# Self-attention and the ternary layers of a perceiver's second level as one part, tile by tile

## The chip, the cores and the metric

The kernel runs on one core of a Trainium2 chip. The metric is the device time of one execution in microseconds (us); lower is better. TensorE is PE in the profile (its weight loads are PEld), VectorE is DVE, ScalarE is ACT, GpSimd is POOL, and SyncE, SP, issues nearly all transfers.

## The reference

Two levels of a perceiver run over tokens x of (8, 64, 512), each with a cross-attention to a context of (8, 1601, 512). Only the end of the second level is touched:

```python
x = x + _L1_xattn_ref(_layernorm(x), ctx_1024, ctx_1024, ...)
x = x + _L1_attn_ref(_layernorm(x), Wq, Wk, Wv, u, v, Wo, bo)
x = x + _L1_ffn_ref(_layernorm(x), w1, b1, w2, b2)
```

`_L1_attn_ref` is a self-attention over the 64 tokens of a batch with 16 heads of 32 and relative positions. The scores are `(q + u) kT + rel_shift((q + v) rT)`, times 32^-0.5, where r are sinusoids of the position. `rel_shift` pads a row of 64 with one zero, reads the rows of 65 as one run of numbers, and takes rows of 64 from it, one row later. A softmax, the values and the product with Wo (plus bo) follow. `_L1_ffn_ref` is two layers, 512 to 2048 to 512, with a gelu between them. Each normalizes its input by its root mean square, rounds it to integer levels of -128 to 127 by the row's largest value, and multiplies with weights rounded to -1, 0 and 1.

## The kernel before

The 512 tokens lie as four tiles of 128 (two batches each) in one buffer x. The tail has two functions that run one after the other.

`l1_attn` (L1545) first fills qv and qu, both 128x4096, with zeros on POOL (L1577, L1578). It normalizes the four tiles (`K.layernorm`: bn_stats, aggregate and variance on DVE at L71, L72, L55, a power on POOL at L56, the result xn on DVE at L76) and turns them into columns xT (xt_ps, L88). Then come the queries of all four tiles at once (q_ps L1587, 512 columns). Two heads share 64 partitions, and one product computes both heads' scores. So a query is stored twice, with zeros in the other head's half: qv on ACT (L1591) and qu on DVE (L1594), in pieces of 32x512 that leave the zeros where the fill put them. `of_pairs` (L1605) multiplies qv with the positions (y_ps); for each tile a zero column is set (L1617), the result is copied to y (two buffers), and four transfers write it to one DRAM buffer, shift, in rows of 65 (L1622). `while_shifting()` then loads the rounded weights w1q and w2q (L1778, L1780). Four transfers for each tile read the rows back in rows of 64 as z (L1637). While this runs, PE computes the keys (k_ps L1645) and values (v_ps L1650) of all tiles. After that, for each tile: `probabilities` (scores s_ps by `of_pairs`, the add of z L1659, max L1663, subtraction L1664, exp on ACT L1665, sum L1666, reciprocal, product L1668), `turn` (pT_ps L1677), `attend` (o_ps L1687, copies oT L1698) and `out` (out_ps L1704, x + bo L1711, x + out_ps L1712). The loop runs one tile ahead: probabilities(t+1) comes before the rest of tile t.

`l1_ffn` (L1806) begins when that is done. It loads the biases b1 and b2, and normalizes all tiles. `first(t)` makes levels of the row (`rms_levels`, L1784 to L1801: the square on ACT, the largest value and the passes on DVE, the root on POOL), turns them (xT_ps L1831), multiplies with w1q (h_ps L1837), scales and adds b1 (h L1840), applies gelu (L1843), and makes levels hq of the 2048 values. `second(t)` turns these (hT_ps L1854), multiplies with w2q (o_ps L1858), scales, adds b2 and x (L1860, L1861) and writes the tile out (L1862). The loop puts first(t) before second(t-1).

Nothing else orders the work by hand. Buffers come from pools, and a pool that is closed gives its memory to the next one; an instruction that writes into such memory waits for the last reader of what lay there. A planner with estimated costs puts the instructions of each engine into one order, and on each engine they run in that order. SP issues transfers in order as well, and an issue that has to wait keeps the later ones back.

What comes just ahead is the end of `l1_xattn`: sums and weighted values (L1465, acc L1456), their reciprocal (L1466) and product oT (L1529), the last tile's out_ps (L1471) and x + out_ps (L1478).

Of the kernel before, what the change touches and what calls it, by code (L numbers as in the profile page):

```python
# [10 lines left out]
F32 = mybir.dt.float32  # L11
# [1204 lines left out]
def l1_xattn(K, x, d):  # L1216
# [7 lines left out]
    with ExitStack() as es:  # L1224
        ep = es.enter_context(tc.tile_pool(name="d_e", bufs=1))
        cp = es.enter_context(tc.tile_pool(name="d_c", bufs=5))
        qp = es.enter_context(tc.tile_pool(name="d_sq", bufs=4))
        wp = es.enter_context(tc.tile_pool(name="d_w", bufs=1))
# [26 lines left out]
        wv = chunked(wp, "L1x_WvT")  # L1255
# [278 lines left out]
def positions():  # L1534

    pos = np.arange(S - 1, -1, -1, dtype=np.float32)
    inv = (1.0 / 10000.0 ** (np.arange(0, DH, 2, dtype=np.float32) / np.float32(DH))).astype(np.float32)
    ang = (pos[:, None] * inv[None, :]).astype(np.float64)
    r = np.concatenate([np.sin(ang), np.cos(ang)], axis=-1).astype(np.float32)
    return {"c_rT": np.tile(r.T, (4, 1))}  # L1540


def l1_attn(K, x, d, while_shifting):

    tc, nc = K.tc, K.nc
    with ExitStack() as es:
        wp = es.enter_context(tc.tile_pool(name="e_w", bufs=1))  # L1550
        rp = es.enter_context(tc.tile_pool(name="e_r", bufs=2))
        dp = es.enter_context(tc.tile_pool(name="e_d", bufs=1, space=DRAM))
        pm = es.enter_context(tc.tile_pool(name="e_ps", bufs=7, space=PSUM))

        qp = tc.tile_pool(name="e_q", bufs=1)
        q_pool = qp.__enter__()

        def weight(name, shape, src, pool=wp):
            t = pool.tile(shape, F32, tag=name, name=name)
            nc.sync.dma_start(t, src)  # L1560
            return t

        def chunked(name, pool=wp):
            return weight(name, [P, DC, D], d[name].rearrange("(c p) n -> p c n", p=P), pool)

        wq = chunked("L1a_Wq", q_pool)
        uv = weight("L1a_uv", [P, 2, DC], d["L1a_uv"])
        rT = weight("c_rT", [P, S], d["c_rT"])
        wk, wv, wo = chunked("L1a_Wk"), chunked("L1a_Wv"), chunked("L1a_Wo")
        bo = weight("L1a_bo", [P, D], bcast_rows(d["L1a_bo"]))  # L1570
        shift = dp.tile([B, 2, DC, 2, S * (S + 1)], F32, tag="shift", name="shift")

        xT = wp.tile([P, DC, B * S], F32, tag="xT", name="xT")

        qu = wp.tile([P, DC, B, 2, S], F32, tag="qu", name="qu")
        qv = q_pool.tile([P, DC, B, 2, S], F32, tag="qv", name="qv")
        nc.gpsimd.memset(qv, 0.0)  # L1577
        nc.gpsimd.memset(qu, 0.0)  # L1578
        xn = q_pool.tile([P, NT, D], F32, tag="xn", name="xn")
        K.layernorm(rp, x, xn)  # L1580
        K.tokens_to_columns(pm, "mm", xn, xT)
        uvs = wp.tile([P, 2, DC], F32, tag="uvs", name="uvs")
        nc.vector.tensor_scalar_mul(uvs, uv, DH**-0.5)
        for c in range(DC):
            ps = pm.tile([P, B * S], F32, tag="mm", name="q_ps")
            for i in range(DC):
                nc.tensor.matmul(ps, lhsT=wq[:, i, ts(c, P)], rhs=xT[:, i, :], start=i == 0, stop=i == DC - 1)  # L1587
            for i in range(4):
                r = ds(DH * i, DH)
                q = ps[r].rearrange("p (b q) -> p b q", b=B)  # L1590
                nc.scalar.activation(  # L1591
                    qv[r, c, :, i % 2, :], q, AF.Identity, bias=uvs[r, 1, c : c + 1], scale=DH**-0.5
                )
                nc.vector.tensor_scalar(  # L1594
                    qu[r, c, :, i % 2, :], q, uv[r, 0, c : c + 1], DH**-0.5, ALU.add, ALU.mult
                )

        def of_pairs(t, qb, rhs, name):

            halves = [pm.tile([P, DC, 2, S], F32, tag="mm", name=name) for _ in range(2)]  # L1600
            for c in range(DC):
                for b in range(2):
                    for j in range(2):
                        r = ds(64 * j, 64)
                        nc.tensor.matmul(  # L1605
                            halves[j][:, c, b, :],
                            lhsT=qb[r, c, 2 * t + b].rearrange("p h q -> p (h q)"),
                            rhs=rhs(r, c, 2 * t + b),
                            start=True,
                            stop=True,  # L1610
                        )
            return halves

        for t in range(NT):
            y = rp.tile([P, 2, DC, 2, S + 1], F32, tag="y", name="y")
            halves = of_pairs(t, qv, lambda r, c, b: rT[r], "y_ps")
            nc.gpsimd.memset(y[:, :, :, :, 0:1], 0.0)  # L1617
            for j in range(2):
                K.copy(y[:, j, :, :, 1:], halves[j])
            for b in range(2):  # L1620
                for h in range(2):
                    nc.sync.dma_start(  # L1622
                        shift[2 * t + b, :, :, h, :].rearrange("j c (q k) -> q (j c) k", k=S + 1),
                        y[ds(64 * h, 64), :, :, b, :].rearrange("q j c k -> q (j c) k"),
                    )

        qp.__exit__(None, None, None)
        while_shifting()
        bp = es.enter_context(tc.tile_pool(name="e_b", bufs=1))
        kT = bp.tile([P, DC, B * S], F32, tag="kT", name="kT")  # L1630
        v = bp.tile([P, NT, D], F32, tag="v", name="v")
        shifted = []
        for t in range(NT):
            z = bp.tile([P, 2, 2, DC, S], F32, tag=f"z{t}", name=f"z{t}")
            for b in range(2):
                for h in range(2):
                    nc.sync.dma_start(  # L1637
                        z[ds(64 * h, 64), b].rearrange("q j c k -> q (j c) k"),
                        shift[2 * t + b, :, :, h, S:].rearrange("j c (q k) -> q (j c) k", k=S),
                    )  # L1640
            shifted.append(z)
        for c in range(DC):
            ps = pm.tile([P, B * S], F32, tag="mm", name="k_ps")
            for i in range(DC):
                nc.tensor.matmul(ps, lhsT=wk[:, i, ts(c, P)], rhs=xT[:, i, :], start=i == 0, stop=i == DC - 1)  # L1645
            K.copy(kT[:, c, :], ps)
        for t in range(NT):
            ps = pm.tile([P, D], F32, tag="mm", name="v_ps")
            for i in range(DC):
                nc.tensor.matmul(ps, lhsT=xT[:, i, ts(t, P)], rhs=wv[:, i, :], start=i == 0, stop=i == DC - 1)  # L1650
            K.copy(v[:, t, :], ps)

        def probabilities(t):

            z = shifted[t].rearrange("p b j c k -> p j c b k")
            p = rp.tile([P, 2, DC, 2, S], F32, tag="p", name="p")
            halves = of_pairs(t, qu, lambda r, c, b: kT[r, c, ds(b * S, S)], "s_ps")
            for j in range(2):
                nc.vector.tensor_add(p[:, j], halves[j], z[:, j])  # L1659
            rows = p.rearrange("p j c b k -> p (j c b) k")  # L1660
            m = rp.tile([P, 16], F32, tag="m", name="m")
            wide = m.unsqueeze(2).to_broadcast([P, 16, S])
            nc.vector.tensor_reduce(m, rows, AX.X, ALU.max)  # L1663
            nc.vector.tensor_sub(rows, rows, wide)  # L1664
            nc.scalar.activation(rows, rows, AF.Exp)  # L1665
            nc.vector.tensor_reduce(m, rows, AX.X, ALU.add)  # L1666
            nc.vector.reciprocal(m, m)
            nc.vector.tensor_mul(rows, rows, wide)  # L1668
            return p

        def turn(p):

            pT = rp.tile([P, 2, DC, P], F32, tag="pT", name="pT")
            for j in range(2):
                ps = pm.tile([P, DC, P], F32, tag="mm", name="pT_ps")
                for c in range(DC):
                    nc.tensor.transpose(ps[:, c, :], p[:, j, c].rearrange("p b k -> p (b k)"), K.ident)  # L1677
                K.copy(pT[:, j], ps)
            return pT

        def attend(t, pT):
            o = [pm.tile([P, DC, 2, S], F32, tag="mm", name="o_ps") for _ in range(2)]
            for c in range(DC):
                for j in range(2):
                    for b in range(2):
                        r = ds(64 * b, 64)
                        nc.tensor.matmul(  # L1687
                            o[b][ds(64 * j, 64), c].rearrange("p h q -> p (h q)"),
# [299 lines left out]
```

## Time and profile before

| | us |
|---|---|
| median of 3 runs | 3331.86 (3327.32 to 3334.03) |
| the profiled execution | 3328.13 |
| its span | 3326.4 |
| end of the last out_ps of the cross-attention | 3106.13 |
| first q_ps | 3119.23 |
| first s_ps | 3171.74 |
| last x + out_ps of the attention (start) | 3239.10 |
| last out-add (start) | 3322.48 |
| from 3106 to 3327: PE, DVE, ACT, POOL busy | 141.11, 120.61, 55.12, 17.71 |
| the same stretch: granted clock | 0.78 |
| mean granted clock of the whole span | 0.974 |

The times in the lower rows are counted from the span's start. A row of the chain or of a timeline gives start, duration, engine, name and line, and how many instructions it holds. In a group's row, the numbers after the bar are the busy time, the mean duration of one instruction in ns, and the engine's idle time just before them with what ended it. A float32 product shows as two rows on PE (16 products of q_ps are 32 rows). The granted clock is the share of full speed that the throttle left to TensorE. Of the kernel's span, 3106 us lie ahead of the change.

### The profile page before, as it was taken

What the parts mean: (1) busy time and instruction counts of PE and PEld (TensorE: products, weight loads), DVE (VectorE), ACT (ScalarE), POOL (GpSimd) and SP (SyncE); (2) the same over time, 40 slices, a digit from 0 to 9 for tenths busy, and PEclk for the clock granted to TensorE, in tenths of its full rate; (3) what the DMA queues carried; (4) which work ended last, traced back from release to release, by engine and by line L of the source; (5) the groups of instructions that cost most, each with busy time, mean ns of one, the idle gap of its engine ahead of it and who ended that gap; (6) DMA issues with size and microseconds to landing.
All of it is one profiled execution on the core that took longest, in us unless ns stands there. A gap on an engine that the chain in (4) does not pass through costs nothing.

```text
span 3326.4 us, 40358 instructions
## 1 busy us (share of the span) xinstructions
PE 3171.3 (95%) x15812; PEld 2145.6 (65%) x15817; DVE 1773.4 (53%) x2931; ACT 837.0 (25%) x1530; POOL 1009.0 (30%) x974
## 2 busy tenths in 40 slices
PE   8999999999999999999899998999999999999765
PEld 6777778888878888875554444655555565555432
DVE  5754556666576656644432235454644545456546
ACT  3232322222233222201021221322223232232213
POOL 5433345443545444420000052313123141221100
PEclk9999999999999999998899998999999999999877
DMA  7255553333364343325388420010000100000430
GB/s 233 75 166 155 171 165 101 101 98 101 111 187 142 99 133 102 91 83 212 134 309 288 162 75 30 10 40 10 31 31 10 40 10 31 21 11 33 95 44 15
DMA packets 314178, 329.03 MB, mean 99 GB/s; under 512 B 35381, under 2 KB 235573, under 8 KB 312837
## 3 DMA queue, kind: packets, MB, share of 16 engines
q1 hardware_dynamic: 310272, 314.88, 30.6%
q10 hardware_dynamic: 3717, 11.57, 0.9%
q8 instruction: 126, 2.06, 0.2%
q14 instruction: 63, 0.52, 0.0%
HBM read 303.30 MB, written 23.10 MB: 98 GB/s over the span
## 4 chain that ended last, share of the span: by engine, by line
PE 87%; DVE 6%; DMA 3%; issue 1%; ACT 1%; POOL 1%; SPq 0%; ACTq 0%; POOLq 0%; DVEq 0%
PE k_ps L1293 11%; PE v_ps L1392 11%; PE x_ps L562 9%; PE x_ps L447 9%; PE s_ps L1406 4%; PE z_ps L562 4%; PE z_ps L447 4%; PE h_ps L1114 3%; PE oe_ps L1141 3%; PE acc L1456 3%; PE y_ps L562 2%; PE y_ps L447 2%; PE sum_ps L1315 2%; PE s_ps L440 1%; PE v_ps L595 1%
## 5 line engine op out<-in xcount | busy, mean ns | idle before, releaser
L1330 POOL TENSOR_TENSOR r<-r,minus_half 128x24 f32<-128x24 f32 x64 | 288.7, 4515 | 748.9 <-DVE r L1326 748.9
L1392 PE MATMUL v_ps<-L1x_WvT,ctxT 128*128 128x512 f32 (+1 forms) x832 | 380.1, 605 | 0.0
L1293 PE MATMUL k_ps<-ctxT,L1x_WkT 128*128 128x384 f32 (+1 forms) x1024 | 375.0, 509 | 0.6 <-ACT o L51 0.6
L447 PE MATMUL x_ps<-qt,ctxT 128*128 128x256 f32 x1152 | 285.6, 381 | 4.9 <-DVE s L412 2.7
L562 PE MATMUL x_ps<-pt,ctx 128*128 128x256 f32 x1152 | 280.4, 381 | 3.1 <-ACT u L510 2.0
L1293 PEld LDWEIGHTS k_ps<-ctxT,L1x_WkT 128*128 128x128 f32 x1024 | 184.0, 189 | 140.2 <-issue 42.8
L1392 PEld LDWEIGHTS v_ps<-L1x_WvT,ctxT 128*128 128x128 f32 (+1 forms) x832 | 149.4, 187 | 170.4 <-issue 165.0
L447 PEld LDWEIGHTS x_ps<-qt,ctxT 128*128 128x128 f32 x1152 | 216.5, 190 | 45.7 <-DVE s L412 7.1
L562 PEld LDWEIGHTS x_ps<-pt,ctx 128*128 128x128 f32 x1152 | 216.4, 189 | 37.0 <-ACT u L510 2.8
L118 POOL TENSOR_TENSOR ctxT<-ctxT 128x256 f32<-128x256 f32 x96 | 80.0, 834 | 404.0 <-DMA ctxT<-in_ctxT 350.2
L1406 PEld LDWEIGHTS s_ps<-qb,kT 64*128 64x128 f32 x1664 | 144.4, 188 | 75.0 <-DVE s L1418 44.1
L428 DVE TENSOR_TENSOR m<-m,s 128x512 f32<-128x512 f32 x176 | 134.5, 764 | 95.0 <-ACT s L426 92.3
L1406 PE MATMUL s_ps<-qb,kT 64*128 64x128 f32 x1664 | 171.6, 288 | 6.7 <-DVE s L1418 6.3
L118 POOL TENSOR_TENSOR ctx<-ctx 128x256 f32<-128x256 f32 x96 | 72.1, 752 | 340.4 <-DMA ctx<-in_ctx 287.1
L1297 ACT ACTIVATE kT<-k_ps,L1x_bk 128x384 f32<-128x384 f32 (+1 forms) x128 | 76.1, 594 | 348.9 <-PE k_ps L1293 343.6
L1326 DVE TENSOR_SCALAR r<-sumT_ps 128x12 f32<-128x12 f32 (+1 forms) x128 | 16.5, 166 | 254.6 <-PE sumT_ps L1323 254.2
L1395 ACT COPY v<-v_ps 128x512 f32<-128x512 f32 (+1 forms) x104 | 60.6, 583 | 336.7 <-PE v_ps L1392 336.7
L1418 DVE TENSOR_TENSOR s<-s_ps,r 128x512 f32<-128x512 f32 x192 | 124.6, 682 | 34.1 <-PE s_ps L1406 33.9
L480 DVE TENSOR_TENSOR s<-s,top_ps 128x1024 f32<-128x1024 f32 (+1 forms) x112 | 123.3, 1137 | 21.2 <-PE top_ps L470 21.2
L1447 DVE TENSOR_TENSOR s<-s,top_ps 128x1664 f32<-128x1664 f32 x64 | 117.9, 1884 | 31.1 <-PE top_ps L1443 31.1
L1426 DVE TENSOR_TENSOR fold<-s 128x1536 f32<-128x1536 f32 x64 | 112.1, 1751 | 37.7 <-ACT s L1448 37.7
L412 DVE SCALAR_TENSOR_TENSOR s<-y_ps,bias,p 128x256 f32<-128x256 f32 x96 | 46.3, 483 | 142.2 <-PE y_ps L447 137.6
(406 smaller groups left out, 5760.6 us busy)
## 6 DMA issues: line engine op xcount, KB each, us to landing
w<-in_L0f_W SPq DMA_DIRECT2D x64, 1024.0 KB, 5.4
ctxT<-in_ctxT SPq DMA_DIRECT2D x192, 256.0 KB, 4.6
ctx<-in_ctx SPq DMA_DIRECT2D x192, 256.0 KB, 3.2
ctxT<-in_ctxT SPq DMA_DIRECT2D x24, 768.0 KB, 4.4
wvT<-in_L0x_WvT SPq DMA_DIRECT2D x16, 1024.0 KB, 7.0
qk<-qk_all SPq DMA_DIRECT2D x15, 1024.0 KB, 6.9
qk_all<-stage SPq DMA_DIRECT2D x32, 384.0 KB, 3.3
wraw<-in_L1f_w1T SPq DMA_DIRECT2D x16, 512.0 KB, 4.2
```

The source lines that it names most:

```text
L118: nc.gpsimd.tensor_add(q[:, 4, :], q[:, 2, :], q[:, 3, :])
L428: nc.vector.tensor_max(self.m, self.m if k else self.s[:, LAST, :], self.s[:, k, :])
L447: nc.tensor.matmul(ps, lhsT=ctxT[i][:, Quarters.LEFT[n], ts(e, P)], rhs=right[n][:, e, :], start=start and e == 0, stop=e == 1, skip_group ...
L480: nc.vector.tensor_sub(s[:, k : k + n], s[:, k : k + n], top.unsqueeze(1).to_broadcast([P, n, HALF]))
L562: nc.tensor.matmul(ps, lhsT=ctx[pair][:, Quarters.LEFT[n], ts(m, P)], rhs=right[n][:, i, :], start=start and i == 0, stop=i == 2, skip_gro ...
L1293: nc.tensor.matmul(ps[:, :n], lhsT=wk[:, e, ts(c, P)], rhs=ctxT[i][:, e, :n], start=e == 0, stop=e == DC - 1)
L1330: nc.gpsimd.tensor_tensor(r[:, at : at + n, :], r[:, at : at + n, :], minus_half[:, :n, :], ALU.pow)
L1392: nc.tensor.matmul(ps[:kn], lhsT=ctxT[i][:, c, ds(at, kn)], rhs=wv[:, c, :], start=c == 0, stop=c == DC - 1)
L1406: nc.tensor.matmul(pair[j][:, i, :], lhsT=kT[c][rows, ts(k0 + i, P)], rhs=qb[rows, c, b].rearrange("p h q -> p (h q)"), start=True, stop=True,
L1418: nc.vector.tensor_mul(out, in_, by)
L1426: nc.vector.tensor_tensor(t, s[:, :, 0:6, :], s[:, :, 6:12, :], op)
L1447: nc.vector.tensor_sub(s[:, j], s[:, j], ps[:, j, :].unsqueeze(1).to_broadcast([P, NK, P]))
```

## The change

`l1_attn` and `l1_ffn` become one function, `l1_tail`; `TernaryWeights` and `rms_levels` stay as they are but stand above it. Its parts:

- **Own halves instead of fills.** A new constant c_own (128x2) holds 32^-0.5 on a head's own half of the partitions and 0 on the other. qu and qv are written over all 128 partitions with it as the scale, so the two fills are gone. Two small products vs = v x own are made on DVE for qv's bias.
- **Two groups.** Tiles 0 to 2 are normalized, turned and projected first (q with 384 columns), then tile 3 (128 columns). The buffers of the first group, pool e_e, lie where l1_xattn's ctxT, v and two others lay; its value weights get a pool of their own, d_v. The small buffers of the statistics, pool e_r, lie over its score buffers. xT is copied on ACT only, and one buffer of xn serves all tiles in turn.
- **Loads.** Wq, uv, own, rT, Wk and Wv are loaded ahead of l1_xattn's end, Wo, bo, w1q, w2q and b1 after it, in SP's queue ahead of the sixteen shift writes; b2 stands behind the first twelve reads of z. Each tile has a DRAM buffer of its own for shift, and three buffers hold z, so that tile 3's is read after the first tile's attention has begun.
- **bo** is added to x on POOL after a group's values.
- **One loop.** A step is: the rest of tile t's attention, probabilities(t+1), layer 2 of tile t-1, layer 1 of tile t. Each tile is normalized for the layers in its own layer 1. PSUM is three banks for xt, q, y and h, three for k, v, s, pT, o, out and o2, and two for the bf16 turns.

```diff
-        nc.gpsimd.memset(qv, 0.0)
-        nc.gpsimd.memset(qu, 0.0)
+        own = weight(ep, "c_own", [P, 2], d["c_own"])
+        for s in range(2):
+            nc.vector.tensor_scalar_mul(vs[:, :, s], uv[:, 1, :], own[:, s : s + 1])
...
-            for i in range(4):
-                r = ds(DH * i, DH)
-                q = ps[r].rearrange("p (b q) -> p b q", b=B)
-                nc.scalar.activation(
-                    qv[r, c, :, i % 2, :], q, AF.Identity, bias=uvs[r, 1, c : c + 1], scale=DH**-0.5
-                )
-                nc.vector.tensor_scalar(
-                    qu[r, c, :, i % 2, :], q, uv[r, 0, c : c + 1], DH**-0.5, ALU.add, ALU.mult
-                )
+                    for s in range(2):
+                        nc.vector.tensor_scalar(
+                            self.qu[:, c, :, :, s, :].rearrange("p n b q -> p (n b) q"),
+                            ps.rearrange("p (b q) -> p b q", q=S),
+                            uv[:, 0, c : c + 1], own[:, s : s + 1], ALU.add, ALU.mult,
+                        )
+                    for i in range(len(self.tiles)):
+                        q = ps[:, ts(i, P)].rearrange("p (b q) -> p b q", b=2)
+                        for s in range(2):
+                            nc.scalar.activation(
+                                self.qv[i][:, c, :, s, :], q, AF.Identity,
+                                bias=vs[:, c, s : s + 1], scale=own[:, s : s + 1],
+                            )
...
+        first = Group(ep, list(range(FIRST)))
+        first.turn()
+        first.queries()
+        for t in first.tiles:
+            positions_of(t, first.qv[t])
+        wk = chunked(big("L1a_Wk"), "L1a_Wk")
+        wv = chunked(big("L1a_Wv"), "L1a_Wv")
+        last = Group(wp, [FIRST])
+        last.turn()
+        last.queries()
+        positions_of(FIRST, last.qv[0])
...
+        for t in range(FIRST):
+            shifted(t)
+        wo = chunked(wp.tile([P, HID], F32, tag="L1a_Wo", name="L1a_Wo"), "L1a_Wo")
+        bo = weight(wp, "L1a_bo", [P, D], bcast_rows(d["L1a_bo"]))
+        w.load(wp)
+        b1 = weight(wp, "b1", [P, HID], bcast_rows(d["L1f_b1"]))
+        b2 = weight(wp, "b2", [P, D], bcast_rows(d["L1f_b2"]))
...
+                nc.gpsimd.tensor_add(x[:, t, :], x[:, t, :], bo)
...
-            nc.vector.tensor_add(x[:, t, :], x[:, t, :], bo)
             nc.vector.tensor_add(x[:, t, :], x[:, t, :], ps)
-        p = [probabilities(0), None, None, None]
-        for t in range(NT):
-            if t + 1 < NT:
-                p[t + 1] = probabilities(t + 1)
-            out(t, attend(t, turn(p[t])))
...
-            if before is not None:
-                second(t - 1, *before)
-            before = got
-        second(NT - 1, *before)
+        rest, got = attention(0), None
         for t in range(NT):
+            rest()
+            if t + 1 < NT:
+                if t == 0:
+                    shifted(FIRST)
+                rest = attention(t + 1)
+            if got:
+                layer2(t - 1, *got)
+            got = layer1(t)
+        layer2(NT - 1, *got)
```

The order that the planner makes of it, engine by engine, is part of what the changed program is, and is told here with the diff. On PE: the last out_ps of the cross-attention, xt_ps of tiles 0 to 2, q_ps, y_ps with some of k_ps between, tile 3's xt_ps, its q_ps among k_ps, y_ps, v_ps, tile 3's k_ps, the last v_ps, s_ps(0), pT(0), o(0), out(0), s_ps(1). Then a step is xT(t), h_ps(t), pT(t+1), o(t+1), hT(t), out(t+1), s_ps(t+2), o2(t). On DVE, the levels hq(t) stand before the copies oT(t+1) and hT(t), and these before x + out_ps(t+1); the statistics of tiles 0 to 2 and xn(0) stand before the last x + out_ps of the cross-attention, and the first bn_stats before its last reciprocal.

## The prediction

> **What bounds the kernel now.** The stage that the diff touches is the tail: from the last projection of the cross-attention (out_ps L1471, done at 3106.13) to the last add (o L1861, done at 3323.2). First I read the page's slices, to see whether TensorE sets the pace there too:
>
> ```profile
> PE   8999999999999999999899998999999999999765
> DVE  5754556666576656644432235454644545456546
> PEclk9999999999999999998899998999999999999877
> ```
>
> Elsewhere PE is full; in the last three slices (83 us each) it is not, and its clock falls. What a change of the tail is worth is therefore read from its waits, not from PE's busy share. Then the busy time in each stretch of the tail (PE, PEld, DVE, ACT, POOL, clock, DMA share, GB/s):
>
> ```profile
> 3106.00:3120.00 14.00, 4.77 (x19) 3.62 (x19) 8.00 (x20) 1.17 (x2) 9.33 (x8) 0.63 0.89 316
> 3120.00:3142.00 22.00, 21.83 (x157) 14.04 (x156) 15.74 (x22) 11.94 (x18) 0.00 (x0) 1.00 0.01 5
> 3142.00:3172.00 30.00, 30.00 (x75) 13.34 (x73) 4.05 (x6) 3.05 (x6) 0.25 (x2) 0.94 1.22 111
> 3172.00:3190.00 18.00, 7.53 (x103) 6.65 (x100) 13.79 (x17) 4.42 (x8) 0.00 (x0) 0.62 0.34 51
> 3190.00:3240.00 50.00, 33.57 (x216) 18.14 (x216) 23.23 (x37) 7.71 (x17) 0.00 (x0) 0.76 0.00 1
> 3240.00:3327.00 87.00, 43.42 (x203) 20.28 (x208) 55.80 (x122) 26.83 (x43) 8.13 (x12) 0.74 0.07 28
> ```
>
> There are three stages. In the head (13 us) POOL works; in the projections (52 us) PE never stops; after them PE and VectorE (DVE) wait for each other in turn. The chain of what ended last names the head's wait and the marks I measure from (start, duration):
>
> ```profile
> 3102.43 3.71 PE out_ps L1471 x8
> 3106.61 3.17 issue
> 3109.77 3.51 POOL qu L1578
> 3113.28 1.14 POOL lt_rstd L56 x2
> 3116.62 1.95 PE xt_ps L88 x8
> ...
> 3119.23 3.71 PE q_ps L1587 x8
> ...
> 3158.01 13.73 PE v_ps L1650 x32
> 3171.74 1.98 PE s_ps L1605 x32
> ...
> 3322.48 0.69 DVE o L1861
> ```
>
> The normalization's rstd waits on POOL behind two zero fills of 3.51 us each. So the tail is: head 3106.13 to 3119.23 = 13.1; projections to 3171.74 = 52.5; attention and layers to 3323.17 = 151.4.
>
> **The head: 13.1 becomes 5.2.** The zero fills go; their work is done by the own-half scale. In the built order the statistics of tiles 0 to 2 and xn(0) stand ahead of x+ on DVE, but the twelve transposes of those tiles stand *behind* the last out_ps on PE. So none of the projection overlaps the cross-attention, although PE is busy for only 9.8 of the 19 us from 3083 to 3102. After out_ps: four transposes of tile 0, x+ 0.69 beside them, xn(1) 0.55, four, xn(2) 0.55, four, ACT's copy 0.59. A group of four took 0.54 warm (pT_ps: eight in 1.09) and 0.98 cold (half of 1.95 above). The sum 3 x 0.6 + 2 x 0.55 + 0.59 is 3.5; with some 0.05 to 0.1 between engines, 3.9. One thing is added ahead: a bn_stats (0.68) stands before DVE's last reciprocal, and an aggregate (0.17) and a second bn_stats (0.68) before the oT multiplies that release out_ps. If the first can't start until the last acc has read its operand (the statistics' buffers lie over the cross-attention's), out_ps comes 1.3 later; if they fill DVE's 0.8 us wait there, some 0.7. I take 1.3. Head 5.2, gain **7.9** (bounds 7 to 9). The two small products uv x own stand in DVE's queue near 3085; their load is issued when w1q's was (3067.9), and small loads here landed 6 us after issue. Were they late, DVE would wait in a stretch that it bounds; at twice that latency it is still early.
>
> **The projections: 52.5 stays.** q and k of three tiles have 384 columns; 32 such rows took 11.0 (k_ps L1293), read as 10.7 without its gaps, against 14.0 (q) and 15.6 (k). The fourth tile's own passes are new: 32 rows of 128 columns each for q and k. No f32 row of that shape is in the trace: by columns 0.4375 x 128/512 = 0.11, by a 128-column transpose 0.136. Taking 0.12, each costs 3.8. Sum: q 10.7, y 9.1, four transposes 0.6, k 10.7, q 3.8, v 13.8, k 3.8 = **52.5** (52 to 53.5). Beside it: qu is 8 x 128x384 plus 8 x 128x128 on DVE instead of 16 x 32x512 at 0.747; even at 0.75 for all it is no more than before. qv on ACT is 32 pieces of 128x128, bounded by 0.36 (a 32x256 copy) to 11.5, under the 20 us of q and y. bo is added on POOL, where a 128x256 add took 0.75 to 0.83, so four of 128x512 some 6: the y fills of tiles 2 and 3 queue behind them, but those y wait for a landed shift anyway.
>
> The positions' round trip must be back when the first scores end, near 3106.1 + 5.2 + 52.5 + 2.0 = 3165.8. Before, the first shift write was issued 22.1 after q_ps began; with q shorter by 3.3 it comes about 3129. SP issues Wo, bo, w1q, w2q and b1 (6.25 MB) *ahead* of the shift writes. At the 316 GB/s of the first row above they take 20 us from 3106, to 3126: just in time. The sixteen writes then took 17.7 on SP's queue and a read landed in 4.2; z(0) is there by about 3153. Cover 12 us; I charge nothing.
>
> **Attention and layers: 151.4 becomes 147.1.** Before, the first x+ comes 26.7 after s_ps(0), since probabilities(1) stands in between; alone it is s 2.0, adds 1.3, max, subtract, sum and product 4 x 1.22, reciprocal 0.25, exp 1.06, turns and copies 2.5, o_ps 2.1, oT 0.8, out_ps 6.5 (its cold price), x+ 0.69 = 22, less 0.5 overlap: 21.5. Then three steps from x+(t) to x+(t+1). DVE's own work in one: probabilities 1.4 + 4 x 1.22 + 0.25, oT 4 x 0.42 and x+ 0.69 = 8.9; the normalization 1.54, first levels 2.55, four h adds 3.0, max 2.29, scalars 0.9, level passes 1.34 + 1.22 = 12.8; hT copies 0.84, o 0.75 + 0.69 = 2.3. Together 24.0. To it come the waits that the in-order queues leave: x+(t+1) for out_ps, which now stands behind hT(t) on PE and behind hq(t) on DVE: 5.2 less the hT copies, 4.0; the first h_ps after xT 1.0; later h_ps 1.0; gelu's end and the rms on POOL 1.7; exp between DVE steps 0.5: 8.2. A step is 32.2. The last tile has nobody beside it: levels 5.6, xT 1.4, first h_ps 1.1, four adds at PE's pace 4.4, gelu, max and levels 6.9, hT 2.2, o2 4.3, o 1.5, and o2(2) in front of xT 1.5: 28.9. Sum 21.5 + 96.6 + 28.9 = **147.0**, gain 4.4. The gain is small because DVE's order is the same work in one line: before, attention steps took 15.0, 16.0, 10.3 and layer steps 20.1, 14.2, 11.5, so a tile of both cost some 29 on average, no more than a step costs now; what goes is the start of the layers (3239.8 to the first out-add at 3276.6, done with nothing beside it).
>
> exp and gelu now alternate, so ACT loads tables five times instead of once; the one gelu load in the trace took 1.283. The load can be issued early while ACT waits; four more cost 0 to 5.1. I take 0.5 a step, inside the 8.2. The Trainium skill, ScalarE: Activation LUTs, "What ACT_TABLE_LOAD costs", puts a drain of about 1380 ns beside it, 2.66 us a switch, and so speaks against alternating; by it, all exposed, the sum would be some 9 higher; no row here shows the drain.
>
> PE's clock is the other unknown. Rows of out_ps took 0.43 before 3106 and 0.65 to 0.81 here:
>
> ```profile
> L1704 PE MATMUL out_ps<-L1a_Wo,oT 128*128 128x512 f32 x32 | 23.3, 894 | 16.4 <-DVE oT L1698 11.9 <-issue 4.5
> ```
>
> Each follows an idle stretch of 2 to 5 us. TensorE: Matmul & The Clock Gate, "Part 1: The HAM clock gate", says that an idle window of some 3.4 us halves the clock; denser steps would by it bring 5.2 down to 3.5. I keep 5.2: PE is still busy for only some 20 of a step's 32 us.
>
> **Sum.** -7.9 + 0 - 4.4 = -12.3. The profiled execution took 3328.13 (span 3326.4 and 1.7 around it), so 3315.8; the median of the three runs is 3.7 above it: **3319.5**, said as 3320. What can be told from no change here is 0.2%, 6.7 us.
>
> **The rivals.**
> - *Warmer.* The mix keeps PE's clock up: out_ps 3.5, h_ps 3.4, short levels' waits; a step is 29. For it: warm rows in the same trace (pT_ps, o_ps at 1.10). Against it: clock 0.74 to 0.76 in both late stretches. -12.3 - 9.6 - 1.5 = -23.4: 3308.
> - *The interleave gives it back.* Each engine runs in order, so h(t) on PE waits behind s(t+1), pT(t+1) behind h(t), out behind hT, x+ behind hq; a step grows to 36.5, with the tables exposed. -12.3 + 12.9 = +0.6: 3332. It decides when a step passes 36.
> - *Slower: the loads before the shifts.* If the 6.25 MB run at the 111 GB/s of the row 3142 to 3172, they end at 3162 instead of 3126. Then writes 17.7, read 4.2 and the landing of the last write, some 4: z(0) at 3188, 22 after the scores. -12.3 + 22.3 = +10: 3342. It decides below 193 GB/s (loads later than 3138.5). For it: b1 is a broadcast and the writes queue behind everything on SP. Against it: that row's traffic was pieces under 512 B; whole weights ran at 316.
> - *Not what it says.* No tile is projected early, by the built order; this is in the forecast already. Had they filled PE's 9 idle us before 3102, some 9 more would go.
>
> **How the numbers follow.** Forecast 0.55 (3311 to 3326), warmer 0.15, given back 0.18, slower 0.12. The range 3305 to 3334 takes in the first three but for their edges, and leaves the slow case out. Faster by over 0.2%: the forecast, the warmer case and 0.03 of the third, 0.73; within: 0.15; slower 0.12.
>
> **What would show it.** Right: no POOL fill in the chain; q_ps some 5 after out_ps; PE full for about 52; p's first add waiting for PE, not for z; x+ every 32, with waits for out_ps of 3 to 5; the last out-add 29 after the last x+. Wrong: p's add released by a DMA; steps of 36 or of 29; xt_ps ahead of out_ps; a DVE wait for uv near 3085. The likeliest miss is the step, three times over: 1 us in it moves the time by 3.

## The result

The changed kernel took 3326.18 us (median of 4; 3325.02 to 3334.37) beside 3332.95 of the kernel before in the same session: ratio 0.9987, 95% interval 0.9965 to 1.0008. So no difference is established, and a gain of 12.3 us, as forecast (a ratio of 0.9963), lies just outside the interval. Its profiled execution took 3325.23 (span 3323.4), 3 us less than that of before. The slices of the page, PE and its clock, look as they did:

```profile
PE   8999999999999999999899998999999999999865
PEclk9999999999999999998899998999999999999977
```

The busy time in stretches of the changed kernel (columns as in the prediction) shows the projections at full clock and the rest as before, PE and DVE each idle for over a third of the time and the clock between 0.70 and 0.77:

```profile
3112.00:3167.00 55.00, 54.44 (x292) 36.03 (x292) 12.56 (x23) 19.04 (x47) 5.34 (x7) 1.00 0.89 183
3167.00:3190.00 23.00, 12.94 (x105) 8.62 (x104) 9.04 (x13) 4.14 (x8) 0.00 (x0) 0.70 0.10 24
3190.00:3256.00 66.00, 39.84 (x230) 20.77 (x231) 43.34 (x82) 24.38 (x39) 3.40 (x6) 0.72 0.01 5
3256.00:3324.00 68.00, 38.40 (x197) 18.85 (x200) 39.51 (x75) 19.83 (x31) 3.68 (x6) 0.77 0.03 12
```

The chain of the changed kernel has no POOL fill, and it has the added statistics, the late out_ps and the new marks:

```profile
3099.39 0.69 DVE lt_st L71
3100.09 0.86 DVE rs L1467
...
3103.24 5.41 PE out_ps L1472 x8
...
3112.56 10.59 PE q_ps L1704 x32
...
3167.16 1.98 PE s_ps L1737 x32
...
3319.60 0.69 DVE o L1916
```

The cross-attention ends some us earlier or later from one execution to the next (its last sum at 3099.6 in both kernels' first profiles, between 3094 and 3108 in the others). From here on I therefore measure from that last sum, here of the kernel before and then of the changed one:

```profile
3099.15 0.47 PE L1465 MATMUL sum_ps<-total,ones 128*64 128x128 f32 x3
```

```profile
3099.18 0.40 PE L1466 MATMUL sum_ps<-total,ones 128*64 128x128 f32 x3
```

**a** is from its end to the start of s_ps(0), **b** from there to the end of the last out-add. Before: a 72.1, b 151.4. Changed: a 67.5, b 153.2. The stretch up to the scores gave 4.6, and the interleave took 1.8.

### The profile page after: what moved, and what is told of

Same layout as the page of the kernel before. It is cut to its first block, busy times and chain, and to the rows that moved or that the text cites. A ratio compares the mean times of both kernels' runs of the same rounds, so it can differ in the third digit from the quotient of the medians.

```text
span 3323.4 us, 40487 instructions
## 1 busy us (share of the span) xinstructions
PE 3180.4 (96%) x15876; PEld 2157.3 (65%) x15881; DVE 1761.9 (53%) x2918; ACT 850.5 (26%) x1564; POOL 1005.8 (30%) x976
## 4 chain that ended last, share of the span: by engine, by line
PE 89%; DVE 5%; DMA 2%; ACT 1%; issue 1%; POOL 1%; ACTq 0%; SPq 0%; POOLq 0%; DVEq 0%
PE k_ps L1294 11%; PE v_ps L1393 11%; PE x_ps L562 10%; PE x_ps L447 9%; PE z_ps L562 5%; PE z_ps L447 4%; PE s_ps L1407 4%; PE h_ps L1114 3%; PE oe_ps L1141 3%; PE acc L1457 3%; PE y_ps L562 2%; PE y_ps L447 2%; PE sum_ps L1316 2%; PE s_ps L440 1%; PE qk_ps L233 1%
## 5 line engine op out<-in xcount | busy, mean ns | idle before, releaser
L1449 ACT ACTIVATE s<-s 128x1664 f32<-128x1664 f32 x64 | 100.7, 1590 | 84.6 <-DVE s L1448 84.4
```

## The experiments

My theory after the first profile: (1) the projection is not early, because the statistics' buffers lie under the cross-attention's scores; (2) the written interleave puts layer 1 of a tile and out of the next into one line, so it gains nothing. The rivals: the table loads, PE's clock alone, or the load order.

Each ratio is to runs of the kernel before in the same session; a and b are of one profiled execution each.

| run | a | b | median us | ratio to before (95%) |
|---|---|---|---|---|
| before | 72.1 | 151.4 | | |
| changed | 67.5 | 153.2 | 3326.18 | 0.9987 (0.9965 to 1.0008) |
| again | 68.7 | 153.0 | 3330.09 (one) | |
| own | 66.3 | 153.6 | 3326.25 | 0.9987 (0.9978 to 0.9997) |
| early | 52.1 | 153.8 | 3312.43 | 0.9949 (0.9931 to 0.9968) |
| noint | 73.9 | 129.3 | 3305.83 | 0.9927 (0.9908 to 0.9947) |
| splita | 73.8 | 146.7 | 3320.58 | 0.9969 (0.9957 to 0.9981) |
| notable | 67.5 | 150.0 | 3323.53 | 0.9972 (0.9961 to 0.9982) |
| lag | 73.9 | 143.1 | 3319.36 | 0.9975 (0.9961 to 0.9989) |
| both | 52.1 | 128.9 | 3286.98 | 0.9865 (0.985 to 0.988) |
| warm2 | 50.4 | 138.9 | 3295.93 | 0.9907 (0.989 to 0.9924) |
| bothoa | 52.1 | 126.5 | 3284.89 | 0.986 (0.984 to 0.9881) |
| bothun | 52.0 | 129.2 | 3286.55 | 0.9878 (0.9849 to 0.9908) |

### early: a pool of its own for the first statistics

```diff
+        st = es.enter_context(tc.tile_pool(name="e_st", bufs=4))
         ep = es.enter_context(tc.tile_pool(name="e_e", bufs=1))
...
-                    K.normalizer(rp, x[:, t : t + 1, :])(0, xn)
+                    K.normalizer(st, x[:, t : t + 1, :])(0, xn)
```

> The changed kernel with one edit: the statistics of the first three tiles get a small buffer pool of their own, opened first, which lies under no score buffer of the cross-attention. In the built order 12 transposes and 14 of the 16 q products of three tiles now stand ahead of the last out_ps. Theory A (the statistics' buffers keep the projection out of PE's 9 idle us, and their wait delays out_ps into a cold clock): out_ps ends near 3106 instead of 3108.65, y_ps begins within 2 us of it instead of 14.5 later, span 3323.4 less 10 to 14. Rival B (DVE sets the pace there, and the new work on DVE, POOL and PE's in-order queue only pushes acc and out_ps back): out_ps later by 5 or more, span less 0 to 5.

Span 3307.9, 15.5 less; a fell by 15.4, b stayed. PE's rows of this run:

```profile
3102.05 3.60 PE L1472 MATMUL out_ps<-L1x_Wp,oT 128*128 128x512 f32 x8
3105.48 1.45 PE L1705 MATMUL q_ps<-xT,L1a_Wq 128*128 128x384 f32 x4
3106.86 1.55 PE L1738 MATMUL y_ps<-c_rT,qv 64*128 64x64 f32 x24
```

28 of the 32 q rows ran ahead of out_ps, in gaps where PE had waited for the softmax; out_ps itself is warm (3.60 instead of 5.41). Theory A holds, with a little more than its upper end. In the changed kernel the first statistics begin when the last acc has read its operand:

```profile
3099.39 0.69 DVE L71 BATCH_NORM_STATS2 lt_st<-x 128x6 f32<-128x512 f32 x1 [0.50 <-PE acc L1457]
```

So the overlap that the second group was made for had been kept from happening by where a few small buffers lay. The new pool also has four buffers of each kind where e_r has two; what the number alone would do was not tried.

### own: the kernel before without the fills

```diff
-        nc.gpsimd.memset(qv, 0.0)
-        nc.gpsimd.memset(qu, 0.0)
...
-                    qv[r, c, :, i % 2, :], q, AF.Identity, bias=uvs[r, 1, c : c + 1], scale=DH**-0.5
+                    qv[:, c, :, s, :], q, AF.Identity, bias=vs[:, c, s : s + 1], scale=own[:, s : s + 1]
```

> The kernel before with the own-half scale alone: no fills, qu and qv written over 128 partitions; nothing else of the change. Theory A (the fills were all that held the head): the two fills of 3.51 go, the head of 13.1 becomes 6 to 7, the rest as before, span 3326.4 less 6 to 7; then this alone gives more than the whole change gave in its profile (3.0). Rival B (normalization of all four tiles takes the fills' place on the chain): less 1 to 3.

Span 3324.6, 1.8 less; a fell by 5.8, b was 2.2 longer. The median ratio is the same as the whole change's. The head, from out_ps' end to q_ps, is 9.4 instead of 13.1, not 6 to 7; and q_ps took 15.42 instead of 14.0, partly at half clock:

```profile
3111.57 2.31 PE L88 MATMUL xt_ps<-ident,xn 128*128 128x128 f32 x8 [3.55 <-DVE lt_var L55]
3114.78 1.97 PE L88 MATMUL xt_ps<-ident,xn 128*128 128x128 f32 x8 [0.90 <-DVE xn L76]
3117.42 15.42 PE L1591 MATMUL q_ps<-xT,L1a_Wq 128*128 128x512 f32 x32 [0.67 <-ACT xT L51]
```

So both theories hold in part: the normalization took the place of half of the fills' 7 us.

### noint: attention first, then the layers, in the written order

```diff
+        p = probabilities(0)
         for t in range(NT):
-            rest()
+            now, p = p, probabilities(t + 1) if t + 1 < NT else None
+            out(t, attend(t, turn(now)))
...
+        for t in range(NT):
+            before, got = got, layer1(t)
+            if before:
+                layer2(t - 1, *before)
```

> The changed kernel with one edit: the written order is the attention of all four tiles and then the layers; what may overlap is left to the planner, which in its order puts layer 1 of tile 0 into the attention. Theory A (steps of 33 to 34 are what in-order queues leave, and the written interleave is worth nothing: 153.1 from s_ps(0) to the end against 151.4 before): span 3323.4 less 0 to 4. Rival B (the interleave is worth what I forecast, 4.4 or more): span 3323.4 plus 4 to 8.

Span 3305.9, 17.5 less: both theories fell short of it. a was 6.4 *longer* (see the clock below), b fell from 153.2 to 129.3. The totals of the two b stretches, first of the changed kernel, then of this run:

```profile
3167.10:3320.30 153.20, 91.08 (x524) 48.22 (x528) 91.89 (x168) 48.34 (x78) 7.07 (x12) 0.73 0.03 9
```

```profile
3173.50:3302.80 129.30, 83.21 (x529) 45.30 (x528) 89.77 (x168) 42.12 (x74) 7.46 (x12) 0.79 0.04 11
```

DVE does the same work (92 and 90 us); it waits for 61 us in the one and for 40 in the other. In this order the planner puts layer 1 of tile 0 into the gaps of the later tiles' attention, and the first out-add comes 9.5 us after the last x + out_ps ends, against 37 in the kernel before (3239.79 to its row here, which stands last):

```profile
3243.50 0.69 DVE L1871 TENSOR_TENSOR x<-x,out_ps 128x512 f32<-128x512 f32 x1 [2.85 <-PE out_ps L1864]
...
3253.68 0.68 DVE L1916 TENSOR_TENSOR o<-o,x 128x512 f32<-128x512 f32 x1
```

```profile
3276.63 0.68 DVE L1861 TENSOR_TENSOR o<-o,x 128x512 f32<-128x512 f32 x1
```

### splita: out ahead of the second levels

```diff
+            rest()
+            got = levels(*half)
             if t + 1 < NT:
                 rest = attention(t + 1)
```

`levels` is layer 1 behind the gelu.

> The changed kernel with one edit: layer 1 is cut after the gelu, and its second level pass is written behind the next tile's out, so that in the built order out_ps(t+1) and s_ps(t+2) stand ahead of hT(t) on PE and oT(t+1) ahead of hq(t) on DVE. Theory A (a step is 33 to 34 because out_ps waits behind hq and hT, and DVE idles 5.7 for it): steps of 27 to 30, span 3323.4 less 9 to 18. Rival B (DVE's chain, or PE's cold clock, fixes the step whatever the order): steps of 32 or more, span less 0 to 4.

b fell by 6.5, short of the 9 to 18 of Theory A, and a grew by 6.3 (the clock again); the span is 4.1 less. Steps of 30.5, 33.6 and 31.4 lie between the theories: out_ps starts earlier, but x + out_ps then waits behind hq and the next normalization behind the softmax. The order inside a step is a part of the loss only.

### lag: the layers one tile further back

```diff
             if got:
-                layer2(t - 1, *got)
-            got = layer1(t)
+                layer2(t - 2, *got)
+            if t:
+                got = layer1(t - 1)
```

> The changed kernel with one edit: the written loop puts the layers one tile further back (attention of t+1 beside layer 1 of t-1 and layer 2 of t-2), so that layer 1 no longer waits for the out_ps that has just ended; tables alternate as before. Theory A (a step is 34 because layer 1 of t, its levels, out_ps of t+1 and x+ form one line from step to step, with DVE idle a third of it): s_ps(0) to the end 135 to 145 instead of 153, span less 8 to 18. Rival (any loop that alternates the two parts costs this, by tables and a cold PE): 150 or more, span less 0 to 3.

b 143.1, inside Theory A's 135 to 145. The span is 3324.5, 1.1 longer and not 8 to 18 less: the last sum came 4.8 later, and a was 6.4 longer in this profile (y_ps at half clock, see below). The ratio is 0.9975 beside 0.9987, with intervals that overlap. With layer 1 no longer hanging on the out_ps that has just ended, 10 of the 24 us between the written loop and 'noint' are back, with tables alternating as before.

### notable: no table loads in the steps

The edit puts `AF.Tanh` for `AF.Gelu`, so this kernel computes something else and serves for its times alone.

> The changed kernel with tanh in place of the gelu, so that ACT's instructions stay as many and as long but no table is loaded in the steps (part of the computation is changed: the activation between the two layers). Theory A (the five table loads are issued while ACT waits, so they cost nothing): span 3323.4 less 0 to 2, steps of 33 to 34. Rival (the loads and a drain beside them stand on the chain of each step): steps shorter by 1.5 to 5, span less 5 to 15.

b fell by 3.2 (steps of 31.9, 33.5 and 33.9). The planner put out_ps ahead of hT here, as in splita, so 3.2 holds the loads and that order together and is not the price of the loads. The changed kernel's ACT rows show why it is small:

```profile
3226.26 0.19 ACT L1620 ACTIVATION_READ_ACCUMULATOR o<-y 128x1 f32 x1
3226.47 1.28 ACT L1822 ACT_TABLE_LOAD   x1
3228.58 1.06 ACT L1822 ACTIVATE p<-p 128x1024 f32<-128x1024 f32 x1 [0.83 <-DVE p L1821]
```

The load follows its forerunner at once, and exp afterwards waits for DVE. The Trainium skill, ScalarE: Activation LUTs, "What ACT_TABLE_LOAD costs", has 1283 ns for the load, as here, and a drain of about 1380 beside it; in these rows no such gap is exposed. Nor is it in 'noint', where the load begins 0.02 us after its forerunner and the gelu follows it at once:

```profile
3222.47 0.63 ACT L1858 COPY oT<-o_ps 32x256 f32<-32x256 f32 x2
3223.12 1.28 ACT L1899 ACT_TABLE_LOAD   x1
3224.41 0.63 ACT L1899 ACTIVATE h<-h 128x512 f32<-128x512 f32 x1
```

### both: early and noint together

> The changed kernel with two edits: the early statistics' pool of the run 'early', and the written order of the run 'noint' (all attention, then the layers). Theory A (the two gains lie in different stretches and add): 52 from the last cross-attention sum to s_ps(0) and 129 from there to the end, as in those two runs, so a span of 3280 to 3288. Rival (the gain of 'noint' came from the cold or warm phase of PE's clock in that run, not from the order): s_ps(0) to the end over 140, span over 3293.

Span 3284.8, a 52.1, b 128.9: the two gains add to within 0.4 us, as Theory A said. The clock phase of 'noint' was not the cause of its gain. The ratio to the kernel before is 0.9865 (0.985 to 0.988), some 45 us.

### again: a second profile of the changed kernel

> The changed kernel once more, for a second profile. Theory A (whether PE's clock halves inside the positions' products is chance from execution to execution): 64 rows of y_ps in either 4.7 or 8.8, and the stretch from q_ps to s_ps(0) 54 to 61, all else within 2. Rival (a cold y_ps belongs to the edits of 'noint' and 'splita'): 4.7 and 54.6 as in the first profile.

The y_ps rows took 4.73 again, out_ps L1472 6.55 (5.41 in the first). That alone doesn't tell theory from rival. All profiles together do better. The 64 y_ps rows of the changed kernel, and then of 'noint' with the window around them:

```profile
3129.15 4.73 PE L1737 MATMUL y_ps<-c_rT,qv 64*128 64x64 f32 x64
```

```profile
3129.31 8.85 PE L1737 MATMUL y_ps<-c_rT,qv 64*128 64x64 f32 x64
```

```profile
3121.00:3138.00 17.00, 17.00 (x104) 13.60 (x102) 2.65 (x4) 4.88 (x13) 0.13 (x1) 0.63 0.71 174
```

The code and the order of this stretch are the same in both, and PE is busy throughout; the granted clock is what differs. Where out_ps L1472 ran cold (changed, again, notable: 5.4 to 6.6), y_ps was warm; where it ran warm (3.70: noint, splita, lag), y_ps was cold, and a 6 us longer; in 'own' q_ps was cold for a part. In the five runs with the early edit out_ps took 3.60 and the 64 y rows 4.7 to 5.0, but the clock fell there as well: in four of them (early, both, bothoa, bothun) it was halved for some 3.4 us at the end of these y rows or just behind them, with PE busy throughout. This is 'early':

```profile
3116.00:3120.00 4.00, 4.00 (x15) 2.78 (x15) 0.00 (x0) 1.06 (x2) 1.06 (x1) 0.57 1.36 93
```

Only warm2 had the full clock from its last sum to its scores, and its a of 50.4 is 1.6 to 1.7 less than the 52.0 to 52.1 of the four, which is what 3.4 us at half clock cost. So the early edit does not do away with the cold stretch; in these profiles it lasted some 3.4 us, as the one at out_ps in the changed kernel's first profile did, and fell behind out_ps. What decides where it falls and how long it lasts was not settled. The rival of 'again' stands too: the three profiles with cold y rows are the three whose loop was written anew.

### warm2: idle products in the gaps

```diff
+            keep_busy(K.ident, pT[:, 0].rearrange("p c k -> p (c k)")[:, :256], 2 if t == 0 else 5)
...
+            if t < NT - 1:
+                keep_busy(hT[:, 0, :], w.w2[:, 0, :], 12)
```

`keep_busy` repeats one product into a bank of the h ring.

> The kernel of the run 'both' with idle products on PE in the gaps ahead of out_ps and of the next tile's xT_ps (2 or 5 float32 products of 256 columns on pT, 12 bf16 ones of 512 on hT, their results unused). Theory A (PE's idle gaps halve its clock, and out_ps, h_ps and o2_ps at half clock stand on the chain): out_ps of the later tiles 3.5 to 4.5 instead of 5.4 to 6.4, h_ps 3.5 to 4.5, s_ps(0) to the end 118 to 125 instead of 129. Rival (the clock doesn't follow such short gaps, or the idle products only keep PE from the next work): 129 or more.

Theory A fell: b 138.9, 10 longer than 'both'. Two rows of out_ps:

```profile
3183.42 6.50 PE L1871 MATMUL out_ps<-L1a_Wo,oT 128*128 128x512 f32 x8 [3.57 <-DVE oT L1865]
...
3212.89 3.67 PE L1871 MATMUL out_ps<-L1a_Wo,oT 128*128 128x512 f32 x8
```

In the first, the idle products ran early in the gap; 3.57 us of waiting for oT remained, and out_ps was as cold as ever. In the second, two rows of h_ps stood right before it, and it was warm. Tile 0 shows the other side: there the idle products filled the gap up to out_ps, and it took 3.67, against 5.37 in 'both', whose row stands last:

```profile
3166.64 2.07 PE L1842 MATMUL busy_ps<-pT,ident 128*128 128x256 f32 x4
3168.85 3.67 PE L1871 MATMUL out_ps<-L1a_Wo,oT 128*128 128x512 f32 x8
```

```profile
3171.37 5.37 PE L1865 MATMUL out_ps<-L1a_Wo,oT 128*128 128x512 f32 x8 [2.15 <-issue]
```

The layers of tile 0 fell behind: their out-add came 91 us after s_ps(0), against 80 in 'both'. So the run shows that these fillers cost more than they gave, not what a PE that stays warm would be worth.

### bothoa and bothun: two small edits on 'both'

In bothoa all copies of oT are on ACT; in bothun the keys' banks come from the y ring.

```diff
-                    (nc.vector.tensor_copy if i % 2 else nc.scalar.copy)(oT[r, :, b, :], o[b][r, :, i % 2, :])
+                    nc.scalar.copy(oT[r, :, b, :], o[b][r, :, i % 2, :])
...
-                ps = pm.tile([P, D], F32, tag="mm", name="k_ps")[:, :n]
+                ps = bank("k_ps")[:, :n]
```

> The kernel of the run 'both' with all eight copies of oT on ACT instead of four on DVE. Theory A (out_ps of later tiles waits for copies that stand in DVE's line behind other work, 5.75, 1.4 and 4.6 us in the run 'both'): the gaps ahead of out_ps shrink to 3 and s_ps(0) to the end is 121 to 127 instead of 128.9. Rival (eight copies of 0.36 in a line on ACT take as long, and DVE wasn't what they waited for): 128 to 132.

b 126.5: the gaps ahead of out_ps are 3.1, 4.1, 1.0 and 3.1. That agrees with Theory A at its upper end; the ratio, 0.986 (0.984 to 0.9881), can't be told from that of 'both'.

> The kernel of the run 'both' with the keys' banks taken from the ring of the positions' banks, so that in the built order no keys stand between the positions' products; single v products of 512 columns do in a few places. Theory A (each change from full-height products to the 64-row ones costs some 0.5, which is what made the projections 54.6 instead of 52.5): the twelve y_ps rows after such a change still cost 0.5 more, their number falls from 4 to 3 and the stretch from the last sum to s_ps(0) is 0 to 1 shorter than 52.1. Rival (the extra time in y_ps was the wait for qv on ACT): 52 or more, with y_ps rows at 0.073 after v as well.

a 52.0. This lies at the edge of both ranges and decides nothing; the rows do. Theory A fell: in this run y rows that follow v cost 0.073 each, no more than others. Twelve rows of the changed kernel did cost 0.123 each; first the changed kernel, then bothun:

```profile
3123.07 1.55 PE L1737 MATMUL y_ps<-c_rT,qv 64*128 64x64 f32 x12
```

```profile
3105.55 0.66 PE L1738 MATMUL y_ps<-c_rT,qv 64*128 64x64 f32 x8
```

## Why the forecast gain was too high

The prediction's range held the time, but at 3305 to 3334 it held the kernel before (3332) as well, so that says little for its terms. Its sign may be right; its size was not: 12.3 forecast, 2.8 in the first profile (223.5 to 220.7 from the last sum to the end), 1.8 in the second. The terms, in us:

| term | forecast | first profile | second |
|---|---|---|---|
| out_ps L1472 ends later | 1.3 | 2.6 | 3.7 |
| out_ps' end to q_ps | 3.9 | 3.9 | 3.9 |
| q_ps to s_ps(0) | 52.5 | 54.6 | 54.5 |
| s_ps(0) to the first x + out_ps done | 21.5 | 22.4 | 24.1 |
| three steps | 96.6 | 101.2 | 99.5 |
| the last tile | 28.9 | 29.5 | 29.5 |

- **The fills** went as forecast; 3.9 from out_ps to q_ps is right. The bn_stats on the chain was right too: it began when acc ended, and rs behind it. What I missed is a cold out_ps: 5.41 and 6.55 instead of 3.70. The longer wait ahead of it (3.66 instead of 2.81) is not enough to explain it: noint, splita and lag have the same 3.66, and there it took 3.70.
- **"No tile is projected early, by the built order"** was right. I priced the lost overlap at some 9; 'early' gave 15.4. The 28 q rows are some 9.3 of it; the 3.9 from out_ps to q_ps went as well, and out_ps was 1.8 shorter. From the first y_ps to the scores both runs took 44.0.
- **The projections**: q 10.6, k of tile 3 3.6 and v 13.8 as summed. y_ps took 11.2 instead of 9.1, which is the miss of 2.1 (k of the first group took 0.6 more, and the other passes made it up). I first took changes between two shapes of product for the cause; bothun speaks against it. Its rival, a wait for qv, fits: ACT wrote qv until 3126.75, over both groups of twelve slow rows. But that was not tested, and the cause stays open.
- **The round trip and the loads**: the first shift write was issued at 3129.24 (forecast: about 3129, though its terms add to 3130), the first add of z waited for PE. The rival with the loads was wrong, and uv was not late.
- **A step** was mis-sized in one term, the wait for out_ps. I took 4.0, from an out_ps of 5.2 (5.2 less the hT copies' 0.84 is 4.4); the four waits were 22.7 together, 5.7 each:

```profile
3212.12 1.23 DVE L1628 TENSOR_SCALAR hq<-h 128x2048 bf16<-128x2048 f32 x1
...
3213.40 1.03 PE L1910 MATMUL hT_ps<-identq,hq 128*128 128x128 bf16 x8 [2.24 <-DVE hq L1628]
...
3215.96 6.02 PE L1864 MATMUL out_ps<-L1a_Wo,oT 128*128 128x512 f32 x8 [0.27 <-DVE oT L1858]
...
3222.02 0.69 DVE L1871 TENSOR_TENSOR x<-x,out_ps 128x512 f32<-128x512 f32 x1 [5.66 <-PE out_ps L1864]
```

  It reads as forecast: hq, hT, out_ps, x, each waiting for the one before; only out_ps is 6.0 to 6.3, cold, though PE had been idle for a mere 0.27 right ahead of it and 2.24 ahead of hT_ps. 1.7 more in each step is 5.1, a little more than the miss of 4.6.
- **What the prediction did not see** is how much was there to win: it treated the step as the fixed price of the interleave, "the same work in one line". 'lag' and 'noint' show that the line comes from the written order, 10 and 24 us of it. The table loads are a small part beside that: taking them out, with another order on PE, gave 3.2.

The likeliest rival was the second, "the interleave gives it back", at steps of 36.5; the steps were 33 to 34, and the rest came from the cold out_ps L1472 (1.3 over its term in the first profile) and y_ps (2.1).

## What to carry to other kernels

Look where a small buffer lies before believing that work is "early": a statistic that overlies a live buffer holds back everything behind it. When a planner fills gaps by itself, write the urgent chain first and let it place the other part; a hand-made alternation, in which each part waits for the other's newest result, can undo the overlap it is meant to make. And on engines that wait for each other, allow for the cold duration of a product behind a wait: the tail's out_ps was forecast at 5.2 and took 6.0 to 6.3 in the steps.

## What was not expected of the hardware

- PE ran at a clock of 0.63 while it was busy all the time (17 of 17 us, 64 rows of y_ps in 8.85 instead of 4.73). The Trainium skill, TensorE: Matmul & The Clock Gate, "Part 1: The HAM clock gate", ties the half clock to idle windows of about 3.4 us; in 'noint' the cold stretch (0.50 in all the 14 us from 3127 to 3141) starts some 14 us after PE's last gap, of 0.68 up to 3110.91, and 22 us after its last one of over 3 us (3.66, ahead of out_ps), inside busy work, which that rule doesn't give. Four of the five runs with the early edit show a shorter one, of some 3.4 us, in busy work too.
- Idle products of 2 us at the start of a gap of 5.6 us did not keep the next product warm (6.50). Where idle products filled a gap up to 0.14 us before it (once), or real work stood right before it, it was warm (3.67).
